# A Mamba layer's scan on one core: the skip term's diagonal on ScalarE, and two steps of the preparation moved by a quarter step

## The chip, the cores and the metric

The kernel runs on one NeuronCore of a Trainium2 chip. Five engines work from queues of their own, in the order in which the program emits: TensorE (PE in the profile, with its weight loads as PEld), VectorE (DVE), ScalarE (ACT), GpSimd (POOL) and SyncE (SP), which here issues the transfers. The metric is the device time of one execution in microseconds; the median of 14 executions of the kernel before is 8227.37 us (8211.84 to 8252.4).

## What is computed

The whole program has four layers; the change lies in layer 0, two Mamba blocks (i = 0, 1) on each of four sequences (b) of 4096 positions and 96 channels, followed by a fusion and a batch normalisation. The core of one block:

```python
h = (seq - mu) * rsqrt(var + EPS) * ln_g + ln_b
xs, z = split(h @ in_w)                       # 192 channels each
xc = silu(conv4(xs) + conv_b)
dbl = xc @ xproj_w                            # dt, B, C
delta = softplus(dt @ dt_w + dt_b)
dA  = exp(delta[..., None] * A)
dBx = delta[..., None] * Bm[:, :, None, :] * xc[..., None]
hstates = scan(h[t] = dA[t] * h[t-1] + dBx[t])
y = einsum('bldn,bln->bld', hstates, Cm) + Dp * xc
seq = seq + (y * silu(z)) @ out_w
```

`Dp * xc` is the skip term. The softplus is computed as relu(x) + ln(1 + exp(-|x|)), with a correction for the rounding of 1 + exp(-|x|).

## The kernel before

A unit is one sequence, one block and one chunk of 512 positions: 4 x 2 x 8 = 64 units, run one after the other. The 192 channels are two halves (`hf`), the 16 states four groups (`nq`), so that a unit has 8 groups, numbered `m`; a group is 128 partitions (32 channels x 4 states) by three quarters (`NG` = 3) of 512 positions. The main loop goes over all groups `v`, and in each over four quarter steps `q`. It is an order written out by hand: each engine gets its instructions in the order in which the loop emits them. Within a quarter step the preparation's pieces come first, then the tasks of `finish`, the `replicate` and `broadcast` transfers, `output` and `collect`, and last the scan.

Per group, on the engines:

- `states_in` (L570, PE): B spread over partitions into the one PSUM buffer `Bb`, for two groups.
- `inputs` (L577, DVE, at q = 3 for the next group): `bt` = xR x Bb, 128 x 1536.
- `decay` (L588, ACT): exp(dR x A) into PSUM (`a_ps`, three buffers), emitted two quarters ahead of its scan.
- `states` (L604, DVE, q = 0, 1, 2): the scan.
- `outputs` (q = 3): ACT copies the last state (L612, `carry`), then POOL multiplies `bt` by C in place (L613).
- `collect` (L630, PE, q = 3, two groups later): sums over the states into `yp`. In the first group of a half the product with the skip term's diagonal (L627) opens `yp`; the diagonal itself (`skips`, L624, the identity times Dp) is made in the first chunk of each block, by DVE: 16 times in all.

Two units ahead, `prepare` makes a unit's inputs. It is a generator; the loop takes one piece (up to the next `yield`) per quarter step, at fixed places: `while taken[w] <= 4 * v + q - PERIOD * (w - 1) + AHEAD`, with PERIOD = 32 quarter steps a unit and AHEAD = 16. In order: centering (L418, PE; copies L423 and L424, ACT), variance (L427, PE), Ln and Exp on ACT (L435, L436), the normalisation's product on DVE (L438), bias (L440, ACT), convolution (L447, PE, 8 matmuls), its copies (L456, ACT), z (L459, PE), the gate of xc (L466, L469, L471 on ACT, the product L472 on POOL), the projection to dbl (L478, PE; copy L482, ACT), dt (L488, PE), the softplus (Abs L495, Exp L497, Relu L498 and L500, 1 + e L502 on ACT; the correction L505 on DVE; Ln L511 on ACT; L512 and L514 on POOL), the transfers of delta and delta x xc to DRAM (L517, L521, with the product L519 on POOL), the gate of z (L524, L526, L531 on ACT; L532 on POOL), and, with L526, the `replicate` transfers (L541) that bring delta and delta x xc back, spread over the partitions (`dR`, `xR`). The second half's `replicate` and the `broadcast` of C (L551) stand in the loop at places of their own.

`finish` (L646 on POOL, L650 and L652 on PE, L654 on ACT; in block 1 also L660, L662 and L664) adds the unit's result to the sequence. All matmuls of `prepare` and `finish` share two PSUM buffers (`mm_ps`).

Of the kernel before, what the change touches and what calls it, by code (L numbers as in the profile page):

```python
# [12 lines left out]
AF = mybir.ActivationFunctionType  # L13
ALU = mybir.AluOpType
# [4 lines left out]
B, C, H, W = 4, 96, 64, 64  # L19
# [320 lines left out]
def layer0(k, X):  # L340

    tc, nc, ins = k.tc, k.nc, k.ins
# [4 lines left out]
    with ExitStack() as es:  # L347
# [46 lines left out]
        def mm():  # L394
            return pm.tile([128, NB], F32, name="mm_ps", tag="mm")
# [18 lines left out]
        def prepare(b, i, ch, st, before):  # L414
# [20 lines left out]
            nc.scalar.activation(p[:C], p[:C], AF.Ln, bias=k.eps5[:C])  # L435
            nc.scalar.activation(p[:C], p[:C], AF.Exp, scale=-0.5)  # L436
            yield
            nc.vector.scalar_tensor_tensor(d, d, k.v(f"ln_g{i}"), p[:C], ALU.mult, ALU.mult)  # L438
            yield
            nc.scalar.activation(h[:, 3:], d, AF.Identity, bias=k.v(f"ln_b{i}"))  # L440
# [2 lines left out]
            ps = []  # L443
# [42 lines left out]
            ps = [mm() for _ in range(2)]  # L486
# [5 lines left out]
            dx = p1.tile([C, 2, T], F32, name="dx")  # L492
            bias = [k.v(f"dt_b{i}{hf}") for hf in range(2)]
            for hf, p in enumerate(ps):
                nc.scalar.activation(e[:, hf], p[:C], AF.Abs, bias=bias[hf])  # L495
            yield
            nc.scalar.activation(e, e, AF.Exp, scale=-1.0)  # L497
            nc.scalar.activation(dx[:, 0], ps[0][:C], AF.Relu, bias=bias[0])  # L498
            yield
            nc.scalar.activation(dx[:, 1], ps[1][:C], AF.Relu, bias=bias[1])  # L500
            for hf, p in enumerate(ps):
                nc.scalar.activation(p[:C], e[:, hf], AF.Identity, bias=k.one[:C])  # L502
            yield
# [52 lines left out]
        carries, bts, Bbs, dec, skips = {}, {}, {}, {}, {}  # L556

        def at(v):

            u, m = divmod(v, NT)  # L560
            return (sts[u], units[u], *divmod(m, 2))
# [55 lines left out]
        def collect(v):  # L617

            st, (b, i, ch), nq, hf = at(v)
            if nq == 0:  # L620
                yp = st["yp", hf] = py.tile([C, T], F32, name="yp")
                if ch == 0:
                    skips[hf] = p1.tile([C, C], F32, name=f"skip{hf}")
                    nc.vector.tensor_scalar(  # L624
                        skips[hf], k.ident[:C, :C], k.v(f"Dp{i}{hf}"), None, ALU.mult
                    )
                nc.tensor.matmul(yp, skips[hf], st["xc"][:, hf], start=True, stop=False)  # L627
            bt = bts.pop(v)
            for q in range(NG):
                nc.tensor.matmul(  # L630
                    st["yp", hf][32 * q : 32 * q + 32],
                    red,
                    bt[:, q],
                    start=False,
                    stop=nq == NQ - 1,
                )
# [32 lines left out]
        with tc.manual_schedule():  # L669
            for _ in pooled(0):  # L670
                pass
            for _ in prepare(*units[0], sts[0], None):
                pass
# [7 lines left out]
            for n in range(2):  # L681
                decay(n)
            preps = [
                prepare(*units[u], sts[u], sts[u - 1]) if u else iter(()) for u in range(len(units))
            ]
            taken, task = [0] * len(units), iter(())
            for v in range(V + 7):
                u, m = divmod(v, NT)
                for q in range(4):
# [25 lines left out]
                    if q == 3 and 0 <= v - 2 < V:  # L715
                        collect(v - 2)
# [12 lines left out]
        scale, shift = batch_norm(k, wp, stats, k.v("bn_g"), k.v("bn_b"))  # L729
# [11 lines left out]
def batch_norm(k, pool, stats, gamma, beta):  # L741

    nc = k.nc
    mv = pool.tile([C, 2], F32, name="bn_mv")
    nc.vector.bn_aggr(mv, stats.rearrange("c b n s -> c (b n s)"))
    sc = pool.tile([C, 2], F32, name="bn_sc")
    nc.scalar.activation(sc[:, 0:1], mv[:, 1:2], AF.Sqrt, bias=k.eps5[:C])
    nc.vector.reciprocal(sc[:, 0:1], sc[:, 0:1])
    nc.vector.tensor_mul(sc[:, 0:1], sc[:, 0:1], gamma)
    nc.vector.tensor_mul(sc[:, 1:2], mv[:, 0:1], sc[:, 0:1])  # L750
    nc.vector.tensor_sub(sc[:, 1:2], beta, sc[:, 1:2])
    return sc[:, 0:1], sc[:, 1:2]
# [1462 lines left out]
```

## Time and profile before

| | us |
|---|---|
| median of 14 executions | 8227.37 |
| the profiled execution | 8248.49 |
| its span | 8246.7 |
| DVE busy, whole span | 5789.2 (70%) |
| PE busy, whole span | 5847.3 (71%) |
| POOL busy, whole span | 4694.9 (57%) |
| ACT busy, whole span | 3901.5 (47%) |
| scan L604, 1536 x 1267 ns | 1872.2 |
| output product L613, 512 x 3443 ns | 1758.1 |
| decay L588, 1536 x 685 ns | 1039.9 |
| input product L577, 512 x 1728 ns | 885.0 |

The span in slices shows where layer 0 lies: in the first 16 of 40 slices, 3300 us, DVE is at 90% or more and POOL at 80%.

```profile
DVE  4999999999999998488664545463446555566555
ACT  4767676767676775333265656564321111111111
POOL 3888888888888886244343434343025545455553
```

Each digit is the busy share of a slice of 206 us in tenths. In a line of the timeline the columns are start, duration, engine, source line, operation, out<-in, shapes, count, and in brackets the idle time before it with what ended it. In a list of waits they are engine, instruction, what it waited for, and the total, the number and the longest of these waits.

### The profile page before, as it was taken

To read this page: it belongs to the slowest core of one execution; us is meant where nothing else is said; L and a number is where in the kernel's file an instruction comes from. 1 tells how busy PE (TensorE), PEld (TensorE's weight loads), DVE (VectorE), ACT (ScalarE), POOL (GpSimd) and SP (SyncE) were. 2 spreads that over 40 slices of the span, in tenths; PEclk is the share of its full clock that TensorE was granted. 3 is DMA by queue.
4 is the path that set the end of the run, shared out by engine and by line. 5 is a ranking of instruction groups with operands and counts; after the bars stand their busy time and mean duration, and the time that the engine had idled before them with its cause. 6 is when DMAs were issued, how large, how long until landed. Compare 5 with 4: busy or idle time off the path is not lost.

```text
span 8246.7 us, 76610 instructions
## 1 busy us (share of the span) xinstructions
PE 5847.3 (71%) x24090; PEld 2705.7 (33%) x24090; DVE 5789.2 (70%) x8127; ACT 3901.5 (47%) x7624; POOL 4694.9 (57%) x2915
## 2 busy tenths in 40 slices
PE   5777777777777776666698989897666556566553
PEld 1222222222222221522364646464543323233221
DVE  4999999999999998488664545463446555566555
ACT  4767676767676775333265656564321111111111
POOL 3888888888888886244343434343025545455553
PEclk8888888888888887887688888888777777777776
DMA  3322233322233223423200001010125344354444
GB/s 100 114 98 98 98 111 101 106 98 98 98 119 100 98 98 104 140 77 83 72 19 19 22 13 28 1 40 16 29 66 150 111 121 130 105 145 114 118 116 122
DMA packets 424411, 720.29 MB, mean 87 GB/s; under 512 B 188149, under 2 KB 190253, under 8 KB 419762
## 3 DMA queue, kind: packets, MB, share of 16 engines
q1 hardware_dynamic: 348710, 480.74, 18.9%
q0 software_dynamic: 73968, 227.47, 9.7%
q10 hardware_dynamic: 1328, 7.20, 0.2%
q8 instruction: 191, 3.13, 0.2%
q14 instruction: 214, 1.75, 0.1%
HBM read 567.04 MB, written 97.82 MB: 81 GB/s over the span
## 4 chain that ended last, share of the span: by engine, by line
PE 37%; DVE 23%; ACT 16%; issue 9%; another core or an unknown queue 8%; POOL 4%; DMA 3%; SPq 1%; DVEq 0%; ACTq 0%; POOLq 0%
PE mm_ps L447 5%; DVE bt L604 5%; DVE bt L577 3%; PE mm_ps L478 3%; PE yp L630 3%; PE sc_ps L1086 3%; ACT a_ps L588 3%; PE pT_ps L1135 2%; POOL xc L472 2%; PE o_ps L1155 2%; DVE prod L2027 2%; DVE sm L2028 1%; PE yb_ps L1933 1%; PE bc_ps L319 1%
## 5 line engine op out<-in xcount | busy, mean ns | idle before, releaser
L604 DVE TENSOR_TENSOR_SCAN bt<-a_ps,carry,bt 128x512 f32<-128x512 f32 x1536 | 1872.2, 1267 | 65.7 <-ACT a_ps L588 10.9
L613 POOL TENSOR_TENSOR bt<-bt,Cb 128x1536 f32<-128x1536 f32 x512 | 1758.1, 3443 | 199.5 <-ACT carry L612 178.2
L2010 POOL DMA_INDIRECT sm<-table,ix x1152 | 1099.5, 954 | 1299.0 <-DVE om L1987 456.7
L588 ACT ACTIVATE a_ps<-dR,w_l_A_log 128x512 f32<-128x512 f32 x1536 | 1039.9, 685 | 614.4 <-DVE bt L604 606.5
L577 DVE TENSOR_TENSOR bt<-xR,Bb 128x1536 f32<-128x1536 f32 x512 | 885.0, 1728 | 25.9 <-DMA xR<-spread 15.9
L2048 PE MATMUL sT_ps<-ident,sd 128*128 128x128 f32 (+1 forms) x896 | 227.2, 377 | 695.3 <-ACT sT L2049 408.8
L630 PE MATMUL yp<-bt,w_c_red 128*32 128x512 f32 x3072 | 596.0, 672 | 12.7 <-POOL bt L613 12.7
L570 PE MATMUL Bb<-dbl,w_c_seln 128*128 128x512 f32 x512 | 355.9, 783 | 326.5 <-DVE bt L577 326.5
L1123 POOL TENSOR_TENSOR p<-p,rs 128x392 f32<-128x392 f32 x384 | 312.0, 840 | 477.7 <-DVE rs L1121 408.6
L447 PE MATMUL mm_ps<-h,Wk 96*128 96x512 f32 x1024 | 481.3, 625 | 138.3 <-issue 85.0
L319 PE MATMUL bc_ps<-xs,w_l_bc 96*128 96x512 f32 x384 | 241.9, 763 | 214.5 <-DVE q L930 214.5
L2048 PEld LDWEIGHTS sT_ps<-ident,sd 128*128 128x128 f32 (+1 forms) x896 | 134.2, 183 | 771.2 <-ACT sT L2049 438.8
L1110 ACT ACTIVATE p<-p,rs 128x196 f32<-128x196 f32 x768 | 342.7, 449 | 82.5 <-DVE rs L1100 82.2
L2049 ACT COPY sT<-sT_ps 128x512 f32<-128x512 f32 (+1 forms) x256 | 122.0, 477 | 523.9 <-PE sT_ps L2048 248.6
L1946 ACT ACTIVATE go<-go_ps,w_l_go_b 18x512 f32<-18x512 f32 x32 | 21.7, 679 | 720.8 <-remote 569.4
L2065 DVE SCALAR_TENSOR_TENSOR z<-yd_ps,vec,yb 96x512 f32<-96x512 f32 x32 | 23.9, 747 | 469.4 <-remote 268.2
L447 PEld LDWEIGHTS mm_ps<-h,Wk 96*128 96x128 f32 x1024 | 198.3, 199 | 427.7 <-issue 427.7
L1933 PE MATMUL yb_ps<-X,w_l_base_w 96*128 96x504 f32 (+3 forms) x576 | 307.8, 698 | 0.3 <-ACT go L1947 0.3
L472 POOL TENSOR_TENSOR xc<-xc,gate 96x1024 f32<-96x1024 f32 x64 | 150.3, 2348 | 260.2 <-ACT carry L612 230.8
L1143 DVE COPY pT<-pT_ps 98x512 f32<-98x512 f32 x256 | 176.0, 687 | 153.2 <-PE pT_ps L1135 145.7
L2027 DVE TENSOR_TENSOR prod<-sm,cws 128x960 f32<-128x960 f32 (+1 forms) x256 | 270.8, 1058 | 6.7
L570 PEld LDWEIGHTS Bb<-dbl,w_c_seln 128*128 128x128 f32 x512 | 89.4, 219 | 553.6 <-DVE bt L577 493.2
(374 smaller groups left out, 13249.8 us busy)
## 6 DMA issues: line engine op xcount, KB each, us to landing
dR<-spread SPq DMA_DIRECT2D x384, 256.0 KB
xR<-spread SPq DMA_DIRECT2D x384, 256.0 KB
Cb<-out_states SPq DMA_DIRECT2D x256, 256.0 KB
spread<-w SPq DMA_DIRECT2D x128, 192.0 KB
spread<-dx SPq DMA_DIRECT2D x128, 192.0 KB
table<-xT SPq DMA_DIRECT2D x256, 96.0 KB
own<-vd SPq DMA_DIRECT2D x512, 36.8 KB
toep<-l_toep SPq DMA_DIRECT2D x12, 1536.0 KB
```

What stands on the lines that cost most here:

```text
L447: nc.tensor.matmul(p, Wk[:, i, t, hf], h[:, t : t + T], start=t == 0, stop=t == 3)
L570: nc.tensor.matmul(Bb, seln[:, nq], st["dbl"], start=True, stop=True)
L577: nc.vector.tensor_mul(bt, st["xR", hf, None], Bb.unsqueeze(1).to_broadcast([128, NG, T]))
L588: nc.scalar.activation(dec[n], st["dR", hf, q], AF.Exp, scale=A[:, i, nq, hf, q : q + 1])
L604: nc.vector.tensor_tensor_scan(t, dec.pop(n), t, carry_of(v)[:, q : q + 1], ALU.mult, ALU.add)
L613: nc.gpsimd.tensor_mul(bt, bt, st["Cb", nq].unsqueeze(1).to_broadcast([128, NG, T]))
L630: nc.tensor.matmul(st["yp", hf][32 * q : 32 * q + 32], red, bt[:, q], start=False, stop=nq == NQ - 1,)
L1110: nc.scalar.activation(ps[n][:, h, i], ps[n][:, h, i], AF.Exp, scale=-1.0, bias=rs[n][:, 0, h, i : i + 1], accum_out=rs[n][:, 1, h, i : i ...
L1933: nc.tensor.matmul(dv[:, r0:r1, c0:c1], w_[:, t], av[b][:ch, 8 * n + r0 + dy : 8 * n + r1 + dy, c0 + dx : c1 + dx], start=t == 4, stop=t == 8,
L2010: nc.gpsimd.indirect_dma_start(sm[u][:, t].rearrange("p q c -> p (q c)"), None, samples[m // NN % 2], bass.IndirectOffsetOnAxis(ap=ix[m][: ...
L2027: nc.vector.tensor_mul(p, v[:, :, 2:4], w_[:, :, 2:4])
L2048: nc.tensor.transpose(p[: e - 128 * q, q - q0], sf[:, 128 * q : e], k.ident)
```

## The change

Three edits, all in layer 0. One more `yield` stands between the normalisation's Exp (L436) and its product (L438), so that the product and all that follows in `prepare` come a quarter step later. In the softplus the Relu of the first half goes a piece up, next to the Abs, the Relu of the second half takes its place, and the yield that stood before it now stands behind it; the number of pieces there stays. And the diagonal of the skip term is made by ACT (Identity with a scale per partition) instead of DVE (a product with a scalar per partition).

```diff
             nc.scalar.activation(p[:C], p[:C], AF.Exp, scale=-0.5)
             yield
+            yield
             nc.vector.scalar_tensor_tensor(d, d, k.v(f"ln_g{i}"), p[:C], ALU.mult, ALU.mult)
...
                 nc.scalar.activation(e[:, hf], p[:C], AF.Abs, bias=bias[hf])
+            nc.scalar.activation(dx[:, 0], ps[0][:C], AF.Relu, bias=bias[0])
             yield
             nc.scalar.activation(e, e, AF.Exp, scale=-1.0)
-            nc.scalar.activation(dx[:, 0], ps[0][:C], AF.Relu, bias=bias[0])
-            yield
             nc.scalar.activation(dx[:, 1], ps[1][:C], AF.Relu, bias=bias[1])
+            yield
             for hf, p in enumerate(ps):
                 nc.scalar.activation(p[:C], e[:, hf], AF.Identity, bias=k.one[:C])
...
-                    nc.vector.tensor_scalar(
-                        skips[hf], k.ident[:C, :C], k.v(f"Dp{i}{hf}"), None, ALU.mult
+                    nc.scalar.activation(
+                        skips[hf], k.ident[:C, :C], AF.Identity, scale=k.v(f"Dp{i}{hf}")
                     )
```

More of the change, by code (lines that the diff above doesn't have):

```diff
@@ L495, in prepare @@
                 nc.scalar.activation(e[:, hf], p[:C], AF.Abs, bias=bias[hf])
+            nc.scalar.activation(dx[:, 0], ps[0][:C], AF.Relu, bias=bias[0])
             yield
             nc.scalar.activation(e, e, AF.Exp, scale=-1.0)
-            nc.scalar.activation(dx[:, 0], ps[0][:C], AF.Relu, bias=bias[0])
+            nc.scalar.activation(dx[:, 1], ps[1][:C], AF.Relu, bias=bias[1])
             yield
-            nc.scalar.activation(dx[:, 1], ps[1][:C], AF.Relu, bias=bias[1])
             for hf, p in enumerate(ps):
```

## The prediction

> **What bounds the kernel now.** The page gives each engine's share. The change touches layer 0 alone, which ends near 3250 us, so I went from the page to VectorE's waits in the first 3300 us, then the costliest groups there, then one regular unit (1000 to 1055 us): its chain of waits, and its instructions engine by engine.
>
> VectorE (DVE) is busy 94% of layer 0 (469 of each 500 us). What it loses (who waited for whom: us in total, times, longest), and one group (busy us, mean ns):
>
> ```profile
> DVE e L505 <- ACT mm_ps L502: 83.6, 54, 30.5
> DVE e L438 <- issue: 62.3, 55, 1.1
> DVE e L438 <- ACT mm_ps L436: 24.8, 8, 7.8
> ```
>
> ```profile
> L624 DVE TENSOR_SCALAR skip<-ident,vec 96x96 f32<-96x96 f32 x16 | 79.1, 4941 | 0.0
> ```
>
> So 1.1 us at each of the two products that the moves concern, and 4.9 us for each diagonal. But VectorE is not alone on the path. The chain of waits of the regular unit (start, us, what):
>
> ```profile
> 1007.85 1.04 ACT gate L469
> 1008.90 0.58 ACT a_ps L588
> 1009.47 0.98 ACT gate L471
> 1010.45 0.10 ACT carry L612
> 1010.55 2.34 POOL xc L472
> ...
> 1012.93 3.78 PE mm_ps L478 x4
> 1016.71 1.89 PE yp L630 x6
> 1018.63 0.58 ACT xc L641
> 1019.21 1.20 ACT a_ps L588 x2
> 1020.41 1.18 ACT e L495 x2
> ```
>
> It runs on over L497, L498, L500 and L502 to L505. It begins at VectorE's first scan of the unit (1005.33) and comes back to VectorE at 1025.05, 1.11 us after that was free. Any delay beyond the slack in this chain is VectorE's delay. GpSimd's (POOL) order and TensorE's (PE) pace in it:
>
> ```profile
> 1003.89 3.45 POOL L613 TENSOR_TENSOR bt<-bt,Cb 128x1536 f32<-128x1536 f32 x1 [1.66 <-ACT carry L612]
> 1010.53 2.35 POOL L472 TENSOR_TENSOR xc<-xc,gate 96x1024 f32<-96x1024 f32 x1 [3.19 <-ACT carry L612]
> 1012.85 6.84 POOL L613 TENSOR_TENSOR bt<-bt,Cb 128x1536 f32<-128x1536 f32 x2
> ```
>
> ```profile
> 1010.67 2.08 PE L570 MATMUL Bb<-dbl,w_c_seln 128*128 128x512 f32 x2 [5.08 <-DVE bt L577]
> 1012.93 3.78 PE L478 MATMUL mm_ps<-xc,w_l_xp 96*128 96x512 f32 x4 [0.19 <-POOL xc L472]
> 1016.64 1.93 PE L630 MATMUL yp<-bt,w_c_red 128*32 128x512 f32 x6
> ...
> 1040.12 7.11 PE L447 MATMUL mm_ps<-h,Wk 96*128 96x512 f32 x16 [2.67 <-issue]
> ```
>
> After an idle 5 us a PE pass takes 1.04 or 0.95 us, where L447 takes 0.44; L630 takes 1.93 us where it takes 1.06 elsewhere in the unit.
>
> **The change, part by part.** Times below are those of this unit less 1000; a step is start to start.
>
> *The added yield* moves all later steps of `prepare` by a quarter against the loop, not only L438. In the order of the built program this changes who is ahead of whom. On POOL the output product L613 of the unit's first state group, so far behind the gate product L472, goes ahead of it, and likewise L613 of the fourth group ahead of L512. On DVE, L438 and L505 go behind a scan (1.18). SP's issues keep their order.
>
> (1) L438: ACT does the same twelve instructions before L436 as now (only permuted), so L436 ends as now against VectorE; the 1.18 us scan ahead of L438 covers the wait of 1.14 but for 0.07. Gain 1.07 us.
>
> (2) The gate product. Now ACT does L466 at 4.82 while it waits for the first scan; afterwards L466 stands behind that wait. From 6.65: decay 0.62, L466 0.95, decay 0.62, L468 0.47, L469 1.05, so the carry copy L612 is at 10.36 and L613 at 10.63 (0.27 later, as 1003.62 to 1003.89). L613 takes POOL 3.40, so L472 runs at 14.03 instead of 10.53, though L471 is done at 11.5. It ends at 16.38; L478 starts at 16.43.
>
> (3) PE. Between L570 (ends 12.7) and L478 it idles 3.7 us. The 83 first matmuls after an idle time over 3.6 us ran at the slow pace but one; after 1.5 to 2.3 us one of 85 did; before L447, after 2.67, 7 of 28. All of L478 is slow now (minimum 1057 ns) and will be: 3.72 us, then L630 1.93, to 22.08. ACT stands at L482 for L478, and behind L482 are L641 and the decays: L641, which needs that L630, starts at 22.13, the decay behind it ends at 23.30. The scan that needs it could run at 21.48: 1.9 us lost.
>
> (4) L488 follows at 22.08. The slow pace lasted from 10.67 to about 18.5, so I take its first half slow (to 23.95), the second not (24.95). ACT: L495's second half to 25.67, the moved Relu 0.57, then the third decay, done at 26.84; its scan could start at 25.74: 1.1 lost. All four passes slow: 0.95 more.
>
> (5) *Rectification.* From L495 to the first L502 ACT still does L495 twice, L497 and both Relus, with one decay more (0.62), so the moved Relu shortens nothing. L497 0.97, L498 0.57, decay 0.62, first L502 0.67: done 29.60, L505 at 29.65, VectorE free since 28.1. Its wait is 1.5 instead of 1.11. The next L577 is at 30.87 instead of 27.46: 3.41 us late.
>
> (6) What is late next. GpSimd: 613 ahead of 512 and the later L505 put L514's DMA at about 39.2 (34.54 now) and L519's at 41.6. The same six issue groups follow on SP 4.6 us later, 2.3 against VectorE; the last xR issue of the first half is near 41.6 now for a product at 51.24, so 7 of 9.6 us remain. Gone, it would cost what the first unit's row shows, up to 15.9 us a time. L447 starts at 43.65 after 2.6 us of idle (L418, L650, L652 and L427 slide too); with L630 and L570, 9.15 us, the next unit's first product can start at 52.9, wanted at 53.1: covered by 0.2. A slow L447 (10.1 instead of 7.1 us) costs 2.7.
>
> (7) *The diagonal.* VectorE loses 16 instructions, 79.1 us. On ACT the nearest rows are 0.19 us (128x3 copy) and 0.67 (96x512); I take 0.3, at a place where ACT waits for L488: nothing on the path (16 x 0.3 = 5 us without that cover). The far end is that it is as slow there: 16 x 4.94, the 79 us given back. The Trainium skill ("SBUF — State Buffer", section "SBUF: two separate sides") holds that VectorE and GpSimd lock a shared port pair for a whole instruction and that ScalarE has its own; by it the stall does not move along. No row here has the operation on ACT.
>
> *Sum.* From L438 to L438 the profile has 62 distances, 104.80 to 3151.36 us: 3046.6. Seven hold two diagonals (57.9 to 58.3 each); three hold a batch mean (51.2); regular ones are 47.39, or 47.8 with L664. After: 47.39 - 1.07 + 3.41 = 49.73, and 50.17 with L664, 31 of each: 3097; three means at 3.3 each: 10; a slow L447 in some six: 16. Together 3123, +77 us on the profiled 8248.49 (span 8246.7), which stood 21 us over the median. On the median: 8227 + 77 = **8304 us**. The diagonals' gain is in it (about 9 us less in each of seven or eight units).
>
> One rule speaks against (3). The Trainium skill ("TensorE: Matmul & The Clock Gate", Part 1) has the clock fall after an idle window of about 3.4 us and rise after as long a busy one. The fall agrees with the rows of idle time; the rise doesn't: here passes were slow 6 us and more into the work (L630 at 16.64). By the rule L630 would be fast at 19.84, each unit 1.9 us shorter, the sum 118 us less: about 8186, an estimate.
>
> **The rivals.**
>
> *PE keeps its pace* (faster). The idle time before L570 shrinks, as a state group's L630 now comes later; if PE is at full pace at L478, its four passes take 2.0, L630 1.0, the decays come in time, and L505 waits 1.45: L577 0.34 late. A unit is 46.7 (47.1), the sum 2934, -113: **8114**. For it: idle before L570 falls from 5.08 to some 3.5. Against it: the 3.7 us of idle that still come before L478, slow in 82 of 83. It decides if L478's mean falls under 0.8 us. 11%.
>
> *The slow pace ends early* (no change or a little faster). L630 at 1.59, the fastest that now follows L478 (0.34 less), and the first half of L488 fast (0.95 less) make 1.3 us a unit; L630 at 1.06 makes 1.8. So 8304 less 81 to 112: **8192 to 8223**. Against it: half of those L630 took 1.93, later after the start of work than here. 17%.
>
> *Slow pace spreads* (slower still). All L488 slow: 62 x 0.95 = 59; L447 slow in the 31 units with the longer idle: 25 more x 2.7 = 68: **8431**. For it: 7 of 28 slow already after 2.67. 8%.
>
> *The diagonal is as slow on ACT*: 8304 + 79 = **8383**; against it: no ACT row over 1.15 us but table loads. 2%.
>
> **How the numbers follow.** The forecast has 62%, with its own range 8250 to 8370 (about 1 us a unit either way). 0.2% of this kernel, 16 us, is about what a measurement tells from no change. Slower: forecast 62, spread 8, diagonal 2, none from the others: 72%. The early end divides into 12 faster and 5 same, as its times pass 8211; with the fast pace 11: faster 23, same 5. The range leaves out the fast pace and the spread, and takes in the early end and the slow diagonal: 8180 to 8390.
>
> **What would show it.** L624 on ACT at about 0.3 us; L438's wait nearly gone; L472 about 3.4 us after L613's start, no longer idle before; L478 still over 1.05 us a pass; new waits of L604 for a_ps L588 of some 3 us a unit (10.9 us in all now); L505's wait near 1.5 us; units of 49.7. I am wrong if L604 does not wait for ACT, or if L478 starts less than 3 us later against the unit's first scan.

## The result, and the profile after

The changed kernel takes 8423.18 us (median of 8 executions, 8409.41 to 8440.62) against 8239.0 us for the kernel before (39 executions): a ratio of 1.0225, 95% interval 1.0211 to 1.0239, 184 us more. The profiled execution has a span of 8421.5 us against 8246.7.

All of it lies in layer 0. As a yardstick I use, as the prediction did, the 62 distances from one normalisation product to the next: 3046.6 us before, 3219.1 after, 172.5 more. From the edits' first line on, a line number of the changed kernel is one higher: L439 is the normalisation's product, L473 the gate product, L479 and L489 the two projections, L506 the softplus' correction, L578 the input product, L605 the scan, L614 the output product, L631 the state sums.

VectorE's waits from 100 to 3450 us (who waited for whom; total, times, longest):

```profile
DVE bt L578 <- PE yp L631: 129.0, 59, 2.5
DVE bt L578 <- issue: 97.1, 45, 3.1
DVE e L506 <- ACT mm_ps L503: 87.0, 62, 1.5
DVE e L439 <- ACT mm_ps L436: 41.0, 62, 0.8
DVE bt L578 <- POOL bt L614: 24.3, 17, 1.4
DVE bt L605 <- ACT a_ps L589: 18.5, 21, 8.9
```

The first two and the fifth are new: the input product L578 hardly waited before. They are two different waits. The first line is the product of a unit's fourth state group, which needs the `bt` buffer of the previous unit's last group. The lines "issue" and "POOL bt L614" are the first product of the next unit; sorted by place, it waits 118.5 us in 61 units, 1.94 each, over the 62 distances (10.0 us in 7 units before). The normalisation's wait has shrunk to 0.66 us but is not gone. VectorE in one unit of the changed kernel, its waiting instructions only:

```profile
1155.67 1.75 DVE L578 TENSOR_TENSOR bt<-xR,Bb 128x1536 f32<-128x1536 f32 x1 [1.43 <-POOL bt L614]
...
1174.22 1.75 DVE L578 TENSOR_TENSOR bt<-xR,Bb 128x1536 f32<-128x1536 f32 x1 [2.29 <-PE yp L631]
...
1181.14 1.30 DVE L506 SCALAR_TENSOR_TENSOR e<-mm_ps,e 96x512 f32<-96x512 f32 x2 [1.43 <-ACT mm_ps L503]
...
1193.79 0.74 DVE L439 SCALAR_TENSOR_TENSOR e<-e,vec,mm_ps 96x512 f32<-96x512 f32 x1 [0.64 <-ACT mm_ps L436]
```

GpSimd in the same unit, whose first scan starts at 1157.53:

```profile
1162.87 3.43 POOL L614 TENSOR_TENSOR bt<-bt,Cb 128x1536 f32<-128x1536 f32 x1 [3.81 <-ACT carry L613]
1166.26 2.35 POOL L473 TENSOR_TENSOR xc<-xc,gate 96x1024 f32<-96x1024 f32 x1
1168.58 3.42 POOL L614 TENSOR_TENSOR bt<-bt,Cb 128x1536 f32<-128x1536 f32 x1
```

L473 comes 8.73 us after the first scan, where it came 5.20 after it before (1010.53 less 1005.33). TensorE:

```profile
1144.73 7.08 PE L448 MATMUL mm_ps<-h,Wk 96*128 96x512 f32 x12 [3.52 <-issue]
1151.75 1.06 PE L631 MATMUL yp<-bt,w_c_red 128*32 128x512 f32 x6
1152.73 1.99 PE L448 MATMUL mm_ps<-h,Wk 96*128 96x512 f32 x4
1154.56 1.02 PE L571 MATMUL Bb<-dbl,w_c_seln 128*128 128x512 f32 x2
...
1168.67 3.78 PE L479 MATMUL mm_ps<-xc,w_l_xp 96*128 96x512 f32 x4 [4.32 <-POOL xc L473]
1172.38 1.71 PE L631 MATMUL yp<-bt,w_c_red 128*32 128x512 f32 x6
1174.02 1.98 PE L489 MATMUL mm_ps<-dbl,w_l_dt_w 128*128 128x512 f32 x4
```

The convolution's (L448) first twelve passes take 7.08 us, 0.59 each instead of 0.44, after 3.52 us of idle time. L571 ends at 1155.58, and the input product of 1155.67 follows at once: it was waiting for L571, though the record names GpSimd. Further down, L631 stands behind L479 and ends at 1174.09; the product of 1174.22 follows.

### The profile page after: what moved, and what is told of

The parts are those of the page before. It is cut to its first block, busy times and chain, and to the rows that moved or that the text cites. A ratio compares the mean times of both kernels' runs of the same rounds, so it can differ in the third digit from the quotient of the medians.

```text
span 8421.5 us, 76671 instructions
## 1 busy us (share of the span) xinstructions
PE 5881.5 (70%) x24090; PEld 2721.0 (32%) x24090; DVE 5727.4 (68%) x8111; ACT 3911.6 (46%) x7640; POOL 4697.5 (56%) x2915
## 3 DMA queue, kind: packets, MB, share of 16 engines
q1 hardware_dynamic: 348710, 480.74, 18.5%
## 4 chain that ended last, share of the span: by engine, by line
PE 27%; DVE 16%; issue 8%; another core or an unknown queue 7%; ACT 7%; POOL 4%; DMA 2%; SPq 1%; DVEq 0%; POOLq 0%; ACTq 0%
PE sc_ps L1087 2%; DVE bt L605 2%; PE pT_ps L1136 2%; PE o_ps L1156 2%; DVE prod L2028 2%; PE yb_ps L1934 1%; DVE sm L2029 1%; PE yd_ps L2061 1%; POOL bt L614 1%; DVE bt L578 1%; PE bc_ps L319 1%; PE m_ps L1545 1%; SPq L1893 1%; PE mm_ps L479 1%
## 5 line engine op out<-in xcount | busy, mean ns | idle before, releaser
L614 POOL TENSOR_TENSOR bt<-bt,Cb 128x1536 f32<-128x1536 f32 x512 | 1759.7, 3442 | 528.2 <-ACT carry L613 276.0
L605 DVE TENSOR_TENSOR_SCAN bt<-a_ps,carry,bt 128x512 f32<-128x512 f32 x1536 | 1863.1, 1267 | 68.3 <-ACT a_ps L589 18.5
L578 DVE TENSOR_TENSOR bt<-xR,Bb 128x1536 f32<-128x1536 f32 x512 | 889.9, 1738 | 266.6 <-PE yp L631 129.0
L448 PE MATMUL mm_ps<-h,Wk 96*128 96x512 f32 x1024 | 614.3, 756 | 220.0 <-issue 120.0
L631 PE MATMUL yp<-bt,w_c_red 128*32 128x512 f32 x3072 | 586.6, 651 | 17.4 <-POOL bt L614 17.4
L571 PE MATMUL Bb<-dbl,w_c_seln 128*128 128x512 f32 x512 | 329.8, 730 | 230.0 <-DVE bt L578 230.0
L448 PEld LDWEIGHTS mm_ps<-h,Wk 96*128 96x128 f32 x1024 | 235.2, 240 | 606.2 <-issue 587.1
L479 PE MATMUL mm_ps<-xc,w_l_xp 96*128 96x512 f32 x256 | 242.0, 1101 | 247.3 <-POOL xc L473 247.3
L2029 DVE TENSOR_TENSOR sm<-sm,cws 128x960 f32<-128x960 f32 (+1 forms) x256 | 267.8, 1046 | 0.0
```

The costliest lines, as they stand in the source:

```text
L448: nc.tensor.matmul(p, Wk[:, i, t, hf], h[:, t : t + T], start=t == 0, stop=t == 3)
L578: nc.vector.tensor_mul(bt, st["xR", hf, None], Bb.unsqueeze(1).to_broadcast([128, NG, T]))
L605: nc.vector.tensor_tensor_scan(t, dec.pop(n), t, carry_of(v)[:, q : q + 1], ALU.mult, ALU.add)
L614: nc.gpsimd.tensor_mul(bt, bt, st["Cb", nq].unsqueeze(1).to_broadcast([128, NG, T]))
L631: nc.tensor.matmul(st["yp", hf][32 * q : 32 * q + 32], red, bt[:, q], start=False, stop=nq == NQ - 1,)
L2029: nc.vector.tensor_mul(v[:, :, 0:2], v[:, :, 0:2], w_[:, :, 0:2])
```

## The experiments

The runs were made on more than one chip. On some of them everything after layer 0 is faster: from the last normalisation product to the end the kernel before takes 5095 us in the profile above, e1 4484 in its own. So each run has its ratio to the kernel before on its own chip, and the sum of the 62 distances, which compares across chips: for every run its difference from the kernel before agrees within 19 us with the difference of the medians on the run's own chip.

| run | ratio (95% interval) | 62 distances, us |
|---|---|---|
| before | 1 | 3046.6 |
| changed kernel | 1.0225 (1.0211 to 1.0239) | 3219.1 |
| e1 diagonal alone | 0.9919 (0.9899 to 0.9938) | 2981.2 |
| e2 swap undone | 1.0157 (1.0140 to 1.0174) | 3146.0 |
| e3 gate late | 1.0217 (1.0200 to 1.0234) | 3193.1 |
| e4 normalisation late | 0.9873 (0.9856 to 0.9889) | 2944.5 |
| e5 filler | 1.0160 (1.0139 to 1.0181) | 3155.7 |
| e6 sums early | 1.0284 (1.0259 to 1.0309) | 3242.3 |
| e7 Relus alone | 0.9956 (0.9938 to 0.9974) | 3011.1 |
| e8 e4 with filler | 0.9909 (0.9881 to 0.9937) | 2981.0 |
| e9 e4, sums early | 0.9895 (0.9875 to 0.9914) | 2960.1 |
| e10 diagonal and Relus | 0.9921 (0.9890 to 0.9951) | 2981.5 |
| e11 yield alone | 1.0200 (1.0160 to 1.0240) | 3209.8 |
| e12 correction late too | 0.9946 (0.9925 to 0.9967) | 2988.9 |
| e13 both swaps undone | 1.0026 (1.0014 to 1.0037) | 3060.6 |
| e14 e12, swap undone | 0.9874 (0.9857 to 0.9891) | 2945.6 |

### One part at a time: e1, e7, e10, e11

e1 is the third hunk of the change alone, e7 the second, e10 both, e11 the added `yield` alone.

> The kernel before, with the diagonal made by ACT and nothing else. Theory: the 16 diagonals stand on VectorE's path; a unit that holds two is 58.1 us against some 47.6, so eight such units give back about 80 us: about 8160 on a median of 8239, and L624 on ACT takes about 0.3 us. Rival: the stall is covered, or the operation is as slow on ACT: 8239, no change.

Measured: 65 us less over the distances. The operation by its tile, in e1:

```profile
L624 ACT ACTIVATE skip<-ident,vec x16: 362/372/387, 134.0 to 2836.0; 96x96 f32<-96x96 f32 x16
```

(nanoseconds: least, median, most.) 0.37 us on ACT instead of 4.9 on VectorE; not all of the 79 us came back, as the softplus' wait, which the stall had covered in these units, reappears (76 us in all, 52 before).

> The kernel before, with the softplus' Relus moved and nothing else. Theory: the same instructions stand on ACT between the Abs and the first 1 + e, so the correction waits as before (1.0 us a unit): no change, within 10 us. Rival (the moved Relu takes 0.57 us out of the chain): 0.57 x 54 = 31 us faster.

Measured: 36 us less, about what the rival said, but not by its way: the softplus' wait is 53.7 us as before (52.1). Two thirds of the gain are in the diagonal: in seven of the eight chunks that make it, the first of the two took 5.78 us before and 2.39 here, 24 us in all. Another 10 us are the waits at the next unit's first product, which are gone. By tile, e7, and below it the yield alone (e11):

```profile
L624 DVE TENSOR_SCALAR skip<-ident,vec x16: 558/3568/4803, 131.0 to 2861.0; 96x96 f32<-96x96 f32 x16
```

```profile
L625 DVE TENSOR_SCALAR skip<-ident,vec x16: 241/256/1065, 131.1 to 3044.0; 96x96 f32<-96x96 f32 x16
```

> The kernel before with the diagonal on ACT and the Relus moved, without the added yield. Theory (moving the Relus shortens nothing by itself; what e7_relu gained lies in the diagonal's stall on VectorE, 2.4 us instead of 5.8 at the first one): as e1_diag, a sum of about 2981, 65 us faster than the kernel before. Rival (the two gains add up): about 2945, 100 us faster.

Measured: 2981.5, e1 to within 0.3 us. With the diagonal off VectorE the moved Relus are worth nothing, as step (5) had it.

> The kernel before with the added yield and nothing else. Theory (the yield carries the whole loss, the two other edits are small gains): a regular unit is as long as in the changed kernel (51.6 us), the waits at the fourth group's input product, at the softplus and at the next unit's first product are all there; the sum lies 40 to 70 us above the changed kernel's 3219, 210 to 240 us over the kernel before. Rival (the moved Relu causes part of the loss together with the yield): under 3219.

Measured: 3209.8. The yield carries the whole loss; the sum is not above that of the changed kernel but 9 us below it, and the intervals of the two ratios overlap. The expected 40 to 70 us are missing because the diagonal no longer stalls: 0.26 us on VectorE, as the line shows. The instruction is the same; its 4.9 us were time in which GpSimd worked. Each of the 16 in the kernel before began while a GpSimd product ran and ended 0.06 to 0.07 us after the end of such a product. In e11 the first diagonal of a chunk meets only the last 0.1 to 1.0 us of a product, behind which GpSimd waits up to 3.0 us for the copy L642, and at the second GpSimd is idle. The 16 take 5 us together, so that beside the yield the move to ACT has 5 us at most to gain.

### The order on GpSimd: e2, e13

```diff
-            nc.gpsimd.tensor_mul(bt, bt, Cb)          # in outputs(v)
+            if v % NT == 0:                           # e13: in (0, 3)
+                held.append(v)
+            else:
+                weigh(v)                              # the same product
...
                             next(preps[w], None)
                             taken[w] += 1
+                    while held and q == 0:
+                        weigh(held.pop())
```

> The changed kernel, with one thing put back: the output product of a unit's first state group is emitted behind the gate product again. Theory (the swap on GpSimd makes the gate product late, and with it the projection and the release of a bt buffer behind it on TensorE): the gate product starts about 6.2 us after the unit's first scan instead of 8.7, VectorE's wait at the input product of the fourth group (127 us in all) is gone, about 8295. Rival (the quarter step itself makes the chain late, the order on GpSimd does not matter): 8423, the wait stays at 2.2 us a unit.

Measured: the wait at the fourth group is gone (0.4 us in all instead of 126.8), so it was the swap and not the quarter step. The gate product starts 6.29 us after the unit's first scan, as expected. But the sum fell by 73 us, not 127: the wait at the next unit's first product rose from 118.5 to 146.8, and the scans of the sixth group waited 21 us instead of 3.

> The changed kernel, with both changes of order on GpSimd put back: the output products of the first and of the fourth state group are emitted behind the gate product and behind L512 (the changed kernel's L513) again. Theory: with the fourth group's product out of its way L513 releases the e buffer in time, so that ACT's Exp of the z gate no longer waits for it (35 us in the changed kernel); the normalisation's wait falls from 0.66 to about 0.1 us (34 us), the convolution starts 0.6 us sooner and the waits of the next unit's first product shrink by as much; the sum falls from the 3146 of e2_swap_undone to 3077 or less (about 30 us over the kernel before), and towards 2985 if the shorter idle time lets TensorE keep its clock. Rival (the quarter step itself makes the normalisation late): 3146, 100 us over the kernel before.

Measured: 3060.6, 158 us less than the changed kernel, and the ratio is 1.0026. VectorE's waits in e13:

```profile
DVE e L506 <- ACT mm_ps L503: 83.4, 60, 1.5
DVE bt L578 <- issue: 76.9, 30, 3.2
DVE bt L578 <- POOL bt L623: 40.4, 28, 1.5
...
DVE e L439 <- ACT mm_ps L436: 6.7, 8, 0.8
```

The normalisation's wait is gone but for 6.7 us. In the changed kernel ACT's Exp of the z gate (L525) had waited for the softplus' difference on GpSimd, which now stood behind the fourth group's product:

```profile
1188.38 1.06 ACT L525 ACTIVATE gate<-sz 96x1024 f32<-96x1024 f32 x1 [0.66 <-POOL dx L513]
```

Both write and read the two buffers with tag "e". L436, and with it L439 and the convolution, came later by that 0.66 us. In e13 ACT has no such wait. Of what is left over e1 (79 us), 45 are the waits at the next unit's first product (117 us, 3 in e1) less the normalisation's wait, which went (7 us, 77 in e1). The convolution was slow in 58 of the 62 units here. The other 34 us lie in smaller waits and in lost overlap.

### Which half of the shift: e3, e4

```diff
-            yield                       # e3: the added one, ahead of L438
...
             nc.scalar.copy(sz[:, 0], zs[0][:C])
             yield
+            yield                       # e3
-            yield                       # e4: this one out, the added one kept
```

> The changed kernel, with the added yield moved from the normalisation's product to behind the copy of z, so that normalisation and convolution stand where they stood before and all from the gate on is a quarter late as in the changed kernel. Theory: the waits at the fourth group's input product (2.2 us) and at the softplus' correction (1.4 us) stay, those at the next unit's first input product (1.9 us a unit, 118 us) fall to the 10 us of before, because the convolution is in its old place and TensorE idles 2.7 us or less ahead of it; the normalisation's wait goes back to 1.14 us (30 us more): about 8345. Rival (the wait at the first input product comes from the late gate, GpSimd or the transfers): about 8425 to 8455.

Measured: the waits at the fourth group (131 us) and the softplus (86) stay, those at the next unit's first product fall to 22.9. The sum fell by 26 us, not by some 80, as the normalisation's wait rose to 1.89 us a unit (117 us in all), not to 1.14. Most of the 0.75 is the wait for the "e" buffer again: ACT's L525 waits 36.0 us for L513 in 55 units, 0.65 each. And the first product's waits did not fall for the theory's reason. The convolution was slow in 49 of the 62 units, after up to 4.1 us of idle time. It starts about 2 us behind the normalisation's product as in the changed kernel, but VectorE has one scan (1.18 us) more to do between that product and the next unit's first one, so that the slow pace is covered there and paid for ahead of the normalisation.

> The changed kernel, with the added yield kept and the yield behind the copy of z taken out, so that normalisation and convolution are a quarter late and all from the gate on stands where it stood before. Theory: no wait at the fourth group's input product (127 us less) and a softplus wait as before (25 to 33 us less); the wait at the next unit's first product stays at some 1.9 us if TensorE's idle time ahead of the convolution stays over 3.2 us (about 8270), and falls to a quarter of it if that idle time falls under 2.9 us (about 8180). Rival (the gate stage causes that wait): it is gone, about 8150, with the convolution still slow.

Measured: no wait at the normalisation at all, none at the fourth group, 57.9 us at the softplus, 40.1 at the first product in 28 units: 102 us less than before, the fastest of all versions with e14; 65 of the 102 us are what the diagonal gives alone (e1). Here the convolution was slow in 13 of the 16 units with a fusion product (L660) in front of it in the first 1700 us, each time after 2.5 us of idle time, and fast in most of the others, after 1.1 to 2.8 us. So the length of the idle time alone does not decide; the next section shows what does.

### The convolution's pace: e5, e8

```diff
             nc.scalar.activation(h[:, 3:], d, AF.Identity, bias=k.v(f"ln_b{i}"))
+            first = mm()
+            if u > 2 and units[u - 3][1] == 0:
+                for _ in range(4):                # e8: 3
+                    nc.tensor.matmul(first, Wk[:, i, 0, 0], before["h"][:, :T], start=True, stop=True)
             yield
```

`first` is then the convolution's own first buffer, and its first product overwrites the filler.

> The changed kernel, with four filler products on TensorE ahead of the convolution (their sums are overwritten by its first product), only in units in which no fusion product stands there (half of them; the other half is the control). Theory: the convolution is slow because TensorE's granted clock falls in the idle time ahead of it, and the slow convolution is what VectorE waits for at the next unit's first input product. So in the filled half a pass of L447 takes 0.44 us instead of 0.59 and more and that wait (1.9 us) is gone, in the other half both stay; the 62 distances sum to about 3160 instead of 3219, 115 us over the kernel before. Rival (the convolution merely starts too late, or the clock does not follow TensorE's own load): no change, 172 us over, or more as the fillers delay it.

Measured: 3155.7. TensorE in two filled units of e5 (L446 is the filler, L455 the convolution):

```profile
1071.85 3.70 PE L446 MATMUL mm_ps<-h,Wk 96*128 96x512 f32 x8
1075.47 5.39 PE L455 MATMUL mm_ps<-h,Wk 96*128 96x512 f32 x12
...
1120.96 3.70 PE L446 MATMUL mm_ps<-h,Wk 96*128 96x512 f32 x8
1125.29 5.39 PE L455 MATMUL mm_ps<-h,Wk 96*128 96x512 f32 x12 [0.63 <-ACT h L441]
```

0.45 us a pass instead of 0.59. The waits at the next unit's first product are down to 53.2 us in 32 units: in the first 1700 us 14 of 15 unfilled units wait 1.4 to 3.0 us, while 14 of 16 filled ones do not wait and two wait 0.5. The convolution starts no sooner in the filled units (38.1 to 38.6 us after the unit's first scan in most) than in the changed kernel (37.9 to 38.3 in the like units). So the wait is the slow pace, and work in TensorE's idle time removes it.

> e4_norm_late with three filler products ahead of the convolution, in the half of the units without a fusion product. Theory (the slow convolution is what is left of the wait at the next unit's first product, 40 us in 28 units): that wait falls to a few us, the 62 distances sum to about 2905 instead of 2945, about 140 us faster than the kernel before. Rival (the convolution's late start is what is left): as e4_norm_late, 100 us faster, or less as the fillers delay it.

Measured: the rival. 2981.0, 36 us more than e4. Most of e4's unfilled units of this kind were fast already (8.3 us from the convolution's first pass to its last); the three fillers run until after `h` is there, and the convolution starts late: 1.1 us of wait in most filled units.

What decides the pace is in the trace too, as the clock granted to TensorE (start:end, us, PE's busy time and instructions, clock, DMA share, GB/s). In every run the clock is 1 or 0.5 and changes only on a fixed grid of 3.41 us. Two convolutions of e4, cut at the grid: one starts at 722.05 after 2.52 us of idle time and is slow, one at 1103.29 after 2.77 us and is fast.

```profile
719.67:723.08 3.41, 1.03 (x3) 1.00 0.86 275
723.08:726.50 3.42, 3.42 (x6) 0.50 0.96 334
...
1098.55:1101.96 3.41, 1.98 (x8) 1.00 0.64 195
1101.96:1105.38 3.42, 2.09 (x5) 1.00 0.89 294
1105.38:1108.79 3.41, 3.41 (x11) 1.00 0.88 276
```

The first idle time lies almost whole in one interval of the grid, and the next interval runs at half clock; the second is shared by two intervals, each still busy for more than half, and the clock stays. In the changed kernel's layer 0, half clock followed on all 163 full-clock intervals in which TensorE was busy for under 45%, on 8 of 23 between 45 and 55%, and on none of the 410 above. Full clock came back after 169 of 182 half-clock intervals that TensorE filled, and after one of the 154 others. So an idle time of 2.5 us costs the pace or not by where it falls on the grid, and one of more than 3.41 us takes at least half of an interval wherever it falls.

### Chain or buffer: e6, e9

```diff
-                    if q == 3 and 0 <= v - 2 < V:
+                    if q == (0 if m == 1 else 3) and 0 <= v - 2 < V:
                         collect(v - 2)
```

> The changed kernel, with the state sums of a unit's last group (L630) emitted at the next unit's (m=1, q=0) instead of (m=1, q=3), so that on TensorE they stand ahead of L570 and L478, not behind them. Theory (a chain from the gate product over L478 and the dt product to the softplus): VectorE's wait for the bt buffer at the fourth group is gone, but the chain behind L478 is shorter only by the 1.7 us that L630 took there, so 1.2 to 1.4 us a unit go, about 75 us, 95 us over the kernel before; if the idle time in front of L570 is short enough for the clock to stay, L478 takes 2.0 instead of 3.7 us and up to 3.6 us a unit go. Rival (the buffer alone is the cause): all of the 2.2 us go and the softplus wait stays at 1.4 us: 135 us, 35 us over the kernel before.

Measured: neither. The wait at the fourth group's product is gone, but the scans of that group now wait for ACT's decays, 156.1 us, the correction starts 23.91 us (median) after the unit's first scan instead of 23.57, and the sum is 23 us higher. VectorE in e6:

```profile
DVE bt L605 <- ACT a_ps L589: 172.5, 132, 8.6
...
DVE e L506 <- ACT mm_ps L503: 90.3, 63, 1.5
```

So the buffer was only the first place where VectorE met the chain. The chain did not get shorter, since the dt product lost its pace (by line, e6 and below it the changed kernel; least, median, most ns):

```profile
L489 PE MATMUL mm_ps<-dbl,w_l_dt_w x256: 677/1057/1222, 79.4 to 3383.3; 128*128 128x512 f32 x128
```

```profile
L489 PE MATMUL mm_ps<-dbl,w_l_dt_w x256: 592/592/1223, 80.0 to 3360.0; 128*128 128x512 f32 x128
```

With the 1.7 us of state sums between L479 and L489 gone, TensorE idles 0.68 us there and L489 runs slow: the interval of the clock's grid is no longer filled.

> The kernel with the added yield kept and the yield behind the copy of z taken out (normalisation and convolution a quarter late, the gate as before), and with the last group's state sums emitted early as in e6_collect_early. Theory: L630 no longer stands between L478 and the dt product, so the softplus wait (1.0 us) falls by what L630 took there, up to 58 us; if the shorter idle time ahead of L570 also keeps TensorE's clock up, L478 is fast and the wait is gone whole: 100 to 160 us faster than the kernel before. Rival (the softplus wait is set by ACT's own work): as e4_norm_late, 100 us faster.

Measured: 2960.1, 16 us more than e4; the softplus' wait is 76.5 us instead of 57.9, and L488's median is 1057 ns here too: the state sums are out of the way, and the pace is lost with them.

### Towards a faster version: e12, e14

e12 is e4 with one more `yield` ahead of the correction L505; e14 is e12 with `weigh` held as in e13, for the fourth group alone.

> e4_norm_late with one more yield in front of the softplus' correction (L505), so that a scan of 1.18 us stands ahead of it as ahead of the normalisation's product. Theory: the wait of 0.96 us there (58 us) is covered, the later transfers still land in time and the convolution keeps its place: a sum of about 2890, 155 us faster than the kernel before. Rival (GpSimd's L512 now goes behind an output product and delta comes 3 to 4 us late; or the later gate of z moves work in front of the normalisation): no gain over e4_norm_late, or a loss, with waits on transfers or at the normalisation.

Measured: the softplus' wait is gone whole, but 44 us were lost against e4: the normalisation waits 0.64 us again (37 us), and the first product 105.8 us in 60 units with a slow convolution. ACT waits 32 us for L513, as in the changed kernel.

> e12_stt_late with the fourth group's output product emitted behind L512 again. Theory: as for e13, ACT's wait for the e buffer goes, the normalisation's 0.64 us (36 us) and 0.6 us of the wait at the next unit's first product (1.76 us, 106 us) go with it: a sum of 2889 to 2920 instead of 2989, 125 to 160 us faster than the kernel before, the fastest so far. Rival: no gain over e12_stt_late (50 us faster than before).

Measured: 2945.6, 43 us less than e12, short of the forecast 2889 to 2920: the normalisation's wait is gone, the first product's is 82.6 us in 41 units, and the fourth group's scans wait 37 us. It equals e4.

## Why the prediction was wrong

The direction, the carrier (the yield) and the first part of the chain (GpSimd's swap, the late gate product, the slow L479) were right, the size was not: 77 us forecast, 184 measured, above the range's end. The forecast names a sign of its own for being wrong, "if L604 does not wait for ACT", and that came: the scans waited 18.5 us for ACT in all, not 3 us a unit, and all units but the first take 50.9 us or more, not 49.7. The terms, in us over the 62 distances, forecast and measured in the profile after:

| step | forecast | measured |
|---|---|---|
| (1) normalisation's product | 0.07 x 62 = 4 | 41.0 |
| (3), (4) fourth group | (1.9 + 1.1) x 62 = 186 | 126.8 + 6.3 |
| (5) softplus' correction | 1.5 x 62 = 93 | 85.6 |
| (6) next unit's first product | 6 x 2.7 = 16 | 118.5 |

**Step (6) failed, by 102 us, more than the whole error of 96 in the sum.** "L447 starts at 43.65 after 2.6 us of idle", slow "in some six" units, was wrong in the idle time and in its consequence. The start was right: 38.27 us after the unit's first scan (38.32 forecast). But the state sums ahead of it ended some 1.0 us sooner than in my replay, with the softplus back 0.7 us sooner. The idle time was 3.3 to 4.2 us in 55 of the 62 units and 2.4 to 2.6 in seven, and the convolution was slow in all of them. With a cover of 0.2 us, each slow convolution went to VectorE, for 1.94 us on average (2.7 forecast). The rival "slow pace spreads" had this in half of the units, with 68 us and a chance of 8%; the rows on idle times in step (3) would have given it the larger part, had the replay been carried with its error of a microsecond. And "7 of 28" was no chance that goes with 2.67 us: in the kernel before, the seven slow ones are those in which 0.56 or more of one interval of the clock's grid was idle, the others have 0.48 at most. e5 shows that the pace, not the late start, makes the wait.

**Step (1) missed 37 us.** "ACT does the same twelve instructions before L436" is right, but one of them, the Exp of the z gate, got a new wait: the "e" buffer that L512 on GpSimd releases late, because of the very swap that the same paragraph names "likewise L613 of the fourth group ahead of L512". I followed that swap to the transfers only. e13 shows it, and e14 against e12 once more.

**Steps (2) to (4): the chain was right, its place and end not.** L614, L473 and L479 came 5.34, 8.73 and 11.14 us after the first scan (forecast, less 5.33: 5.30, 8.70, 11.10). VectorE stopped not at the fourth group's scan but ahead of it, at its input product, which needs the buffer that L631 behind L479 frees. That gains nothing: with the buffer free sooner, the scans behind it waited for the same chain (e6). But L489 ran at full pace (592 ns), not half slow as step (4) took it: the 1.1 us did not come, and the fifth group's product, the one behind the softplus, was late by 2.7 instead of 3.4 us. This gave back 53 us of the error, which is luck: two steps were off in opposite directions. The clock shows why step (4) misjudged the pace. In the kernel before it was at half from 1008.25 to 1018.49, three intervals, of which the last (from 1015.08) was the first that TensorE filled. So the passes that were slow 6 us into the work do not refute a rise after 3.4 us of work, for which the prediction took them: the time counts from the grid, and it was the unbroken interval that counted.

**Step (5)** held: the softplus waits 1.40 us (forecast 1.5), and the moved Relus are worth nothing (e10).

**Step (7)** had the right price on ACT (0.37 us; 0.3 forecast; the stall did not move along), and alone the edit gains 65 us. In the changed kernel it gains 5 us at most, because the yield had already removed the stall (e11). The forecast's sum was built from new units, so this did not enter its error.

The table explains 79 of the 96 us by which the sum of the distances (3219 against 3123) was missed. Of the other 17, some 13 are lost overlap: where VectorE does not wait, an instruction starts a little before the one ahead of it ends, 131 us in all before and 118 after. The rest I have not assigned.

What stays open: why the clock fell in 8 of the 23 intervals that were busy for 45 to 55%, and why 13 filled intervals did not bring it back.

## What to carry to other kernels

A yield added in a generator that is stepped against a fixed loop moves every later instruction on every queue; list each pair that changes places, and follow each swap to all that it releases: data, pool buffers, PSUM. Here one yield cost 2% by two swaps on GpSimd and by idle time on TensorE, while the same delay limited to normalisation and convolution (e4) was 1.3% faster than the kernel before, 0.8 of it by the diagonal (e1). Price an instruction that stalls with the neighbour that makes it stall: when the order changes, the price may vanish by itself, and gains measured alone do not add.

## What the runs showed of the hardware

- A VectorE product of 96x96 by a scalar took 0.24 to 1.07 us in e11 and 4.8 us (median) in the kernel before, with the same operands. All 16 in the kernel before began while a GpSimd product ran and ended 0.06 to 0.07 us after such a product's end; the eight in e11 that began with GpSimd idle took 0.26 us. On ACT it took 0.36 to 0.39 us wherever it stood.
- Taking useful work off TensorE can slow what follows: without the 1.7 us of L630 between them, the dt product after the xc projection ran at 1057 ns instead of 592 (e6, e9), and eight filler passes made the convolution's passes 0.45 us instead of 0.59 (e5).
- The clock granted to TensorE moves between 1 and 0.5 on a grid of 3.41 us, by TensorE's work in the interval before (163 of 163 falls under 45% busy, none of 410 over 55%, in the changed kernel). Idle time of 2.4 us was enough for a fall, and 2.77 us was not always (e4).
- In the changed kernel the clock was at half from 1163.49 to 1173.73; L479 took up work at 1168.67, and L489 ran at full pace from 1174.02. The Trainium skill ("TensorE: Matmul & The Clock Gate", Part 1) gives about 3.4 us of sustained work for the rise; the trace agrees if they count from the grid, as the interval from 1170.32 to 1173.73 was the first that TensorE filled.
